# The first image's Gram sums: outer rows turned on TensorE, inner rows in 32-channel blocks on VectorE

## The chip, the cores and the metric

The kernel runs on one core of one Trainium2 chip, in one launch. The metric is the device time of that core in microseconds: the median of the runs shown. One further run was taken with the hardware profiler; every view below is of that one.

## The reference, cut to what matters

Eight images `x[b]` of 256 channels and 96 x 96 pixels, all float32, pass two layers, each added to its input:

- layer 0: group norm; three 1x1 convolutions give q, k, v; a 2-D Fourier transform of each; per head (8 heads of 32 channels) q and k are normalized over all frequencies and give a 32 x 32 attention, whose softmax is taken on the real and on the imaginary part; the result is applied to v, transformed back, its absolute value taken, and a last 1x1 convolution applied;
- layer 1: group norm, then linear attention with softplus features.

The kernel never forms the spectra of q and k. It needs, per image, the 256 x 256 sums over pixels of x times x, and of x times the point-mirrored x (row h, column w against row -h, column -w, modulo 96). From those sums the norms and logits of layer 0 follow. This study is about how those two sums are formed for image 0.

## The kernel before

**Two arenas.** `arena0` and `arena1` (128 partitions, two channel halves of 9232 floats) change roles from image to image: `x_of(b)` holds the image, `y_of(b)` the rotated copy that `rotate` makes.

**Sums.** `products` multiplies a pair of turned rows (pixels on partitions, channels along the free axis): for e = row + mirrored row and o = row - mirrored row it adds e'e into `acc[0]` and o'o into `acc[1]`, four matmuls for each block of pixels. A pair of image rows has 96 pixels to a row, so the pixels must first be brought onto the partitions. Two routes exist.

- `first_sums`, image 0: 24 units of two rows each and a last one of one row. `mirrored(u)` (ScalarE) reverses the mirrored rows, `turn(u)` makes eight TensorE transposes into PSUM and two copies (ScalarE, VectorE) into a *place* in an arena, `pair(u)` makes e (GpSimd) and o (VectorE), and `products` is called twice with 96 of 128 partitions filled. Image rows come in naturally, channels on partitions, with long contiguous rows (`first_loads`). The turned rows stay in their places until `rotate(0)` has used them.
- `pair_sums(b)`, images 1 to 7: `load_grouped(b, v)` fetches eight rows and their mirrors with 32 channels on partitions for each of four row pairs, eight DMAs of 192 KB; `turn_blocks(u)` turns them in 32 x 32 blocks on VectorE, two for each u, and after an odd u writes the turned rows out to DRAM (`xtd`, one DMA of 1536 KB) and asks for the group after next; `pair(u)` makes e and o; three calls of `products` for each u use all 128 partitions. A last u = 12 holds row 48 alone (`xtm`). The turned rows have one buffer, `turned(b)`, so the next even u waits until the write to `xtd` is done. `rotate(b)` fetches the turned rows back.

**Rotation.** `rotate(b)` makes 49 steps of TensorE matmuls with a small matrix `tm` (`load_r`: one DMA of 159 KB from the table `rx` for two units of rows), evicted in turn by ScalarE and VectorE. A step is taken whenever the driver at the end of the kernel says `next(turns)`; eleven are taken while image 0's sums are still running, the others between the links of `attention(0)`.

**Order.** Nothing is scheduled automatically: each engine executes its instructions in the order in which the driver's generators emit them, and all DMAs are issued by SyncE's queue (SP) in that order. For image 0 the driver goes round `first_sums`; from the eleventh round it also calls `next(parts)`, that is `tables()` and in it `load_small()`, which issues 28 small loads (`b12`, `bkq4`, `tcol`, `wkq0`, `b3col`, `wo`), and from the sixteenth it also calls `next(turns)`.

Of the kernel before, what the change touches and what calls it, by code (L numbers as in the profile page):

```python
# [73 lines left out]
def two_layer_kernel(ctx: ExitStack, tc: tile.TileContext, x, w1t, b1, w2t, b2, w3, b3, wot, temp,  # L74
# [252 lines left out]
    def finish(stage):  # L327
        for _ in stage:
            pass
# [3 lines left out]
    def release(key):  # L333
        if next(held.get(key, iter(())), None) is None:
            held.pop(key, None)

    N2 = 2 * C
    places = [(0, 0, 3328), (0, 0, 4864), (0, 1, 4864),
              *((0, k, o) for k, o in ((0, 1280), (0, 2304), (0, 5888), (0, 6912), (1, 5888), (1, 6912))),
              *((1, k, 0) for k in range(KC)), *((0, 1, o) for o in (1280, 2304)), *((1, k, o) for o in (8192, 1024, 7168, 2048, 6144, 3072) for k in range(KC))]  # L340

    def place(u):

# [3 lines left out]
    def first_loads():  # L347

        nc.sync.dma_start(out=t0[:, 0:2 * W], in_=tmat[0, :, W:3 * W])
        x0 = x_of(0)  # L350

        def load(lo, hi):
            nc.sync.dma_start(out=x0[:, :, lo * W:hi * W], in_=x_v[0, :, :, lo * W:hi * W])

        for lo, hi in ((0, 4), (H - 4, H), (4, 8), (H - 8, H - 4), (8, 16), (H - 16, H - 8)):
            load(lo, hi)
        yield
        load(16, 24)
        yield
        for lo in (H - 24, 24, H - 32):  # L360
            load(lo, lo + 8)
        yield
        for t in range(4, NT // 2):
            load(8 * t, 8 * t + 8)
            load(H - 8 * t - 8, H - 8 * t)
        yield

    def first_sums():

        b = 0  # L370
        x0 = x_of(0)
        acc = [acc_tile(f"acc{c}_{b}") for c in range(2)]
        CB = C + 2
        NU = H // 4
        eos, gs = {}, {}

        xr = x0[:, :, 0:HW].rearrange("p k (h w) -> p k h w", w=W)

        def mirrored(u):

            nr = 2 if u < NU else 1
            g = two.tile([P, CH], F32, tag="v16", name=f"g_{b}_{u}")[:, 0:KC * nr * W].rearrange("p (k r w) -> p k r w", k=KC, r=nr)
            h = H - 2 * u
            parts = [(g, xr[:, :, h:h - nr:-1])] if u else [(g[:, :, r:r + 1], xr[:, :, (H - r) % H:(H - r) % H + 1]) for r in range(nr)]
            for to, v in parts:
                nc.scalar.copy(to[:, :, :, 1:W], v[:, :, :, W - 1:0:-1])
                nc.scalar.copy(to[:, :, :, 0:1], v[:, :, :, 0:1])
            return g

        def turn(u):  # L390

            t = place(u)
            nr = 2 if u < NU else 1
            g = gs.pop(u)
            if u < NU:
                gs[u + 1] = mirrored(u + 1)
            for c in range(2):
                pt = ps_tile(f"x_{b}_{u}_{c}")
                for r in range(nr):
                    for k in range(KC):  # L400
                        v = g[:, k, r, :] if c else xr[:, k, 2 * u + r, :]
                        nc.tensor.transpose(pt[0:W, r * C + k * P:r * C + (k + 1) * P], v, ident)
                copy = nc.vector.tensor_copy if c else nc.scalar.copy
                copy(t[:, c * N2:c * N2 + nr * C], pt[0:W, 0:nr * C])

        def pair(u):

            nr = 2 if u < NU else 1
            eo = ring_tile(f"eo_{b}_{u}")[0:W, 0:2 * nr * CB].rearrange("p (q c n) -> p q c n", q=nr, c=2)
            f, g = (place(u)[:, c * N2:c * N2 + nr * C].rearrange("p (r n) -> p r n", r=nr) for c in range(2))  # L410
            e, o = (eo[:, :, c, 1:C + 1] for c in range(2))
            nc.gpsimd.memset(eo[:, :, :, 0:CB:CB - 1], 1.0 if u < NU else R2)
            if u in (0, NU):
                nc.gpsimd.memset(eo[:, 0, :, 0:CB:CB - 1], R2)
                nc.vector.tensor_scalar_mul(o[:, 0], g[:, 0], R2)
                nc.vector.scalar_tensor_tensor(e[:, 0], in0=f[:, 0], scalar=R2, in1=o[:, 0], op0=ALU.mult, op1=ALU.add)  # L416
                nc.vector.scalar_tensor_tensor(o[:, 0], in0=f[:, 0], scalar=R2, in1=o[:, 0], op0=ALU.mult, op1=ALU.subtract)
                e, o, f, g = (v[:, 1:] for v in (e, o, f, g))
            if u < NU:
                nc.gpsimd.tensor_add(e, f, g)  # L420
                nc.vector.tensor_sub(o, f, g)
            eos[u] = eo

        gs[0] = mirrored(0)
        turn(0)
        turn(1)
        pair(0)
        yield
        for u in range(NU + 1):
            if u + 2 <= NU:  # L430
                turn(u + 2)
            if u < NU:
                pair(u + 1)
            eo = eos.pop(u)
            for q in range(2 if u < NU else 1):
                products(acc, eo, q, W, u == 0 and q == 0, u == NU)
            yield
        s0[b] = acc, weights(b)

    def weights(b):  # L440

# [13 lines left out]
    def pair_sums(b):  # L455

        ready = {}

        def prepare(key, step):
            if key in (("turn", 10), ("pair", 10), ("turn", 11), ("turn", 12)):  # L460
                held[key] = step()
            else:
                finish(step())
# [2 lines left out]
            ready[u] = pair(u)  # L466
            yield

        acc = [acc_tile(f"acc{c}_{b}") for c in range(2)]
        CB = C + 2  # L470

        wrap = two.tile([P, 2 * NB8], F32, tag="wrap", name=f"wrap_{b}")
# [48 lines left out]
                (nc.gpsimd if b and u % 2 else nc.vector).tensor_sub(o, ft, gt)  # L521
            return eo, nq, np_

        finish(turn_blocks(0))
        finish(make(0))
        finish(turn_blocks(1))
        if b:
            finish(make(1))
        yield
        for u in range(NG + 1):  # L530
            eo, nq, np_ = ready.pop(u)
            for q in range(nq):
                if q == 0 and u < NG and u + 1 not in ready:
                    prepare(("pair", u + 1), lambda u=u: make(u + 1))
                if q == 1 and u + 2 <= NG:
                    prepare(("turn", u + 2), lambda u=u: turn_blocks(u + 2))
                if (u, q) == (NG - 1, 1):
                    wl = weights(b)
                products(acc, eo, q, np_, u == 0 and q == 0, u == NG)
                yield  # L540
# [188 lines left out]
    def rotate(b):  # L729
# [5 lines left out]
        def load_r(i):  # L735
            tm = tm_tile(f"tm_{b}_{i}")
            o = (TR if i < NP else 1) * (W + 2) + P - W
            v = rx[i][:, 0:o]
            if b == 0 and i < NP:
                v = v.rearrange("(j q) w -> q j w", q=NQ)  # L740
            nc.sync.dma_start(out=tm[:, 0:o], in_=v)
            return tm
# [3 lines left out]
        slots = [area[0:W, k, o + 4 * C * i:o + 4 * C * (i + 1)].rearrange("p (c m) -> p c m", c=2)  # L746
                 for k, o, n in ((0, LO, 3), (1, LO, 3), (0, LO + 12 * C, 1)) for i in range(n)]
        assert LO + 16 * C <= AW and LO + 12 * C <= LO + NS * CH + 2 * CH
        xts, tms = {}, {}
        at_ = [0]  # L750

        def fetch():

            i = at_[0]
            at_[0] += 1
            if i > G * NG // 2:
                return
            h = 2 * i
            if h // TR not in tms:
                tms[h // TR] = load_r(h // TR)  # L760
            if b == 0:
                xts[i] = place(i).rearrange("p (c m) -> p c m", c=2)
                return
            xts[i] = slots[i % len(slots)]
            if h == N:
                nc.sync.dma_start(out=xts[i][:, 0, 0:C], in_=xtm)
            else:
                v, a = divmod(i, G)
                nc.sync.dma_start(out=xts[i], in_=xtd[:, v, 32 * a:32 * a + 32].rearrange("c j (q m) -> (j q) c m", q=NQ))
# [407 lines left out]

    E = mybir.EngineType
    with tc.manual_schedule(engines={E.PE, E.DVE, E.Pool, E.SP, E.Activation}):
        sums, loads, parts = first_sums(), first_loads(), tables()  # L1180
        fetch, turns = rotate(0)
        next(loads)
        next(parts)
        next(loads)
        next(parts)
        next(loads)
        next(parts)
        finish(loads)
        for i, _ in enumerate(sums):
            if i > 9:  # L1190
                next(parts, None)
            if i > 14:
                next(turns)
        finish(mix(0, attention(0), turns))
        for b in range(B):
            sums = pair_sums(b + 1) if b + 1 < B else iter(())
            weave(images(b), sums)
            weave(layer1(b), sums)
            if b + 1 < B:
                fetch, turns = rotate(b + 1)  # L1200
                mixed = mix(b + 1, attention(b + 1), turns)
                output(b, *l1.pop(b), fetch, sums, mixed)
                finish(mixed)
            else:
                output(b, *l1.pop(b))
# [50 lines left out]
```

## Time and profile before

| what | value |
|---|---|
| median of 3 runs | 2520.37 us (2518.79 to 2521.01) |
| profiled execution, device time | 2519.43 us |
| its span, first to last instruction | 2517.7 us |
| TensorE busy | 2489.2 us (99%) |
| VectorE, ScalarE, GpSimd busy | 70%, 46%, 34% |
| granted TensorE clock, mean | 0.993 |
| image 0's sums on TensorE | from 4.81 us (first transpose) to 102.8 us (last product) |

The span is the profiled execution without 1.7 us around it; the profiled time lies 0.9 us below the median. A TensorE that is 99% busy in the page says that it was hardly ever without an instruction, not that it was at its peak. The stage of the change is the first 104 us of 2517.7, so busy shares of the whole page say little of it: it has to be read in the timeline.

### The profile page before, as it was taken

The page shows a single profiled execution, that of the slowest core. Times are in us where ns is not written, and L with a number is a line of the kernel's source. Part 1 is how long each engine was busy: PE and PEld are TensorE (multiplying, and loading weights), DVE is VectorE, ACT ScalarE, POOL GpSimd, SP SyncE. Part 2 cuts the span into 40 slices and gives each one's busy share as a digit, 9 for nine tenths or more (in the row PEclk, how much of TensorE's full clock was granted, in tenths as well). Part 3 has the DMA queues.
Part 4 walks back from the last instruction along what each step waited for, and adds up shares of the span by engine and source line. Part 5 has one row for each costly group of instructions (what it writes and reads, how often), then busy time and mean ns, then how long its engine had stood idle before and what let it go on. Part 6 is the DMA issues. An engine that isn't in the chain of part 4 may idle for free. (4 is left out here: it accounts for less than half of the span.)

```text
span 2517.7 us, 42049 instructions
## 1 busy us (share of the span) xinstructions
PE 2489.2 (99%) x15936; PEld 1758.1 (70%) x15936; DVE 1774.8 (70%) x3448; ACT 1161.3 (46%) x2045; POOL 860.6 (34%) x820
## 2 busy tenths in 40 slices
PE   9999999999999999999999999999999999999998
PEld 8975777667686667856678566785667757677546
DVE  4467776687856877578775787757877578766776
ACT  3344364443545435354453534435354453634553
POOL 4124513245133442234331353413524135142411
PEclk9999999999999999999999999999999999999997
DMA  7134719456192663917549264683637736296004
GB/s 230 35 129 95 183 62 318 154 126 179 64 340 103 158 153 105 335 70 166 135 161 337 42 167 105 216 284 63 163 86 268 232 63 189 60 312 213 1 7 151
DMA packets 264645, 394.07 MB, mean 157 GB/s; under 512 B 37400, under 2 KB 194300, under 8 KB 264444
## 3 DMA queue, kind: packets, MB, share of 16 engines
q1 hardware_dynamic: 264444, 391.38, 52.5%
q8 instruction: 127, 2.08, 0.3%
q14 instruction: 74, 0.61, 0.1%
HBM read 246.99 MB, written 144.32 MB: 155 GB/s over the span
## 5 line engine op out<-in xcount | busy, mean ns | idle before, releaser
L844 PE MATMUL z<-arena,mz 128*128 128x384 f32 (+1 forms) x2304 | 591.9, 488 | 0.0
L894 POOL TENSOR_TENSOR e<-e 128x768 f32<-128x768 f32 x192 | 348.5, 1815 | 552.7 <-ACT e L893 526.4
L852 PE MATMUL po<-e,wo 128*128 128x384 f32 x1536 | 527.5, 487 | 1.7 <-ACT e L895 1.7
L844 PEld LDWEIGHTS z<-arena,mz 128*128 128x128 f32 (+1 forms) x2304 | 310.1, 163 | 234.7 <-issue 50.5
L450 PEld LDWEIGHTS acc<-eo 128*128 128x128 f32 (+1 forms) x2464 | 390.0, 190 | 86.6 <-issue 32.3
L450 PE MATMUL acc<-eo 128*128 128x257 f32 (+3 forms) x2464 | 441.4, 330 | 1.6 <-DVE eo L416 1.6
L852 PEld LDWEIGHTS po<-e,wo 128*128 128x128 f32 x1536 | 290.0, 190 | 204.7 <-ACT e L895 7.2
L889 DVE TENSOR_TENSOR e<-z,xT 128x768 f32<-128x768 f32 x384 | 361.2, 950 | 64.7 <-PE z L844 63.4
L783 PEld LDWEIGHTS y<-tm,arena 96*128 96x128 f32 x3072 | 360.4, 192 | 38.5 <-issue 23.4
L783 PE MATMUL y<-tm,arena 96*128 96x128 f32 x3072 | 379.0, 278 | 0.4 <-DMA arena<-xtd 0.4
L893 ACT ACTIVATE e<-e 128x1536 f32<-128x1536 f32 x192 | 284.5, 1482 | 173.3 <-DVE e L889 171.1
L895 ACT ACTIVATE e<-e 128x768 f32<-128x768 f32 x192 | 162.0, 844 | 381.9 <-POOL e L894 379.9
L854 DVE TENSOR_TENSOR arena<-arena,po 128x384 f32<-128x384 f32 x384 | 209.4, 551 | 180.4 <-PE po L852 180.1
L520 POOL TENSOR_TENSOR eo<-arena 128x768 f32<-128x768 f32 x77 | 157.3, 2042 | 412.6 <-DVE arena L493 312.1
L1149 POOL TENSOR_TENSOR arena<-arena,po 128x384 f32<-128x384 f32 x180 | 178.2, 1009 | 196.2 <-ACT po L1148 166.8
L789 DVE COPY arena<-y 128x384 f32<-128x384 f32 (+1 forms) x192 | 104.7, 545 | 137.4 <-PE y L783 135.9
L789 ACT COPY arena<-y 128x384 f32<-128x384 f32 (+1 forms) x200 | 94.5, 473 | 227.8 <-PE y L783 204.8
L295 DVE BATCH_NORM_STATS2 st<-arena 128x6 f32<-128x384 f32 x384 | 195.2, 548 | 0.6
L1148 ACT COPY po<-o 128x384 f32<-128x384 f32 x180 | 78.0, 482 | 191.0 <-PE o L1140 187.6
L493 DVE STREAM_TRANSPOSE arena<-arena 128x768 f32<-128x768 f32 x168 | 155.2, 956 | 10.2 <-DMA xtd<-arena 8.1
L1009 PE MATMUL xT<-ident,arena 128*128 128x128 f32 x1152 | 144.1, 275 | 1.3 <-ACT xT L1012 1.3
L1009 PEld LDWEIGHTS xT<-ident,arena 128*128 128x128 f32 x1152 | 127.1, 141 | 19.0 <-issue 16.5
(242 smaller groups left out, 2544.7 us busy)
## 6 DMA issues: line engine op xcount, KB each, us to landing
arena<-in_x_dram SPq DMA_DIRECT2D x106, 768.0 KB
out_dram<-arena SPq DMA_DIRECT2D x192, 384.0 KB
xtd<-arena SPq DMA_DIRECT2D x42, 1536.0 KB
arena<-xtd SPq DMA_DIRECT2D x168, 384.0 KB
arena<-in_x_dram SPq DMA_DIRECT2D x329, 192.0 KB
tm<-rx SPq DMA_DIRECT2D x96, 159.0 KB
wl<-in_w1t_dram SPq DMA_DIRECT2D x8, 256.0 KB
wl<-in_w2t_dram SPq DMA_DIRECT2D x8, 256.0 KB
```

The costliest lines, as they stand in the source:

```text
L295: nc.vector.bn_stats(out=st[:, k, c, :], in_=x_of(b)[:, k, c * CH:(c + 1) * CH])
L450: nc.tensor.matmul(acc[c][:, m * (C + 1):m * (C + 1) + C + 1 - m * P], lhsT=eo[0:np_, q, c, 1 + m * P:1 + (m + 1) * P], rhs=eo[0:np_, q, c ...
L783: nc.tensor.matmul(pu[:, o:o + P], lhsT=xt[:, s, k * P:(k + 1) * P], rhs=tm[:, n:n + P], start=True, stop=True)
L789: copy(y[:, :, :, g:g + nr, :], v.rearrange("p k r (f w) -> p k f r w", f=2))
L844: nc.tensor.matmul(out[:, 0:CH].rearrange("p (h q) -> p h q", q=PR), lhsT=columns(mz, k, c, j), rhs=yz[:, k, f, :, o:o + PR], start=(k == ...
L852: nc.tensor.matmul(po[:, 0:CH], lhsT=wo[:, k, m * P:(m + 1) * P], rhs=e[:, k, :], start=(k == 0), stop=(k == KC - 1))
L854: nc.vector.tensor_add(x[:, m, n], x[:, m, n], po[:, 0:CH])
L889: nc.vector.tensor_add(e[:, 2 * c:2 * c + 2, :].rearrange("p t (q h) -> p t q h", h=H), pz[:, 0:CH].rearrange("p (h q) -> p q h", h=H).uns ...
L893: nc.scalar.activation(e, e, AF.Square)
L894: nc.gpsimd.tensor_add(e[:, 0:2, :], e[:, 0:2, :], e[:, 2:4, :])
L1009: nc.tensor.transpose(pt[:, j * C + k * P:j * C + (k + 1) * P], x[:, k, o:o + P], ident)
L1149: nc.gpsimd.tensor_add(x[:, m, r], x[:, m, r], t)
```

## The change

Image 0 now takes both routes. The outer 24 rows and their mirrors go the way of `first_sums` (12 units); the inner rows go the way of `pair_sums(0)`, beginning at u = 6 and adding into the same `acc`. Natural rows of the upper half lie at a shifted address (`LO`), so that the front of the arena is free for the grouped rows. Three places move. In `rotate(0)`, units 12 to 24 are fetched back from `xtd` and `xtm` into five slots. The driver interleaves the first steps of `pair_sums(0)` with the last four rounds of `first_sums`, and small loads and rotation steps with the rest. The diff, with the plain renamings left out:

```diff
@@ places, first_loads
+    V0 = 3
...
-              *((1, k, 0) for k in range(KC)), *((0, 1, o) for o in (1280, 2304)), *((1, k, o) for o in (8192, 1024, 7168, 2048, 6144, 3072) for k in range(KC))]
+              (1, 0, LO), (1, 1, LO), (1, 0, 8192)]
+    NU = V0 * G
...
         def load(lo, hi):
-            nc.sync.dma_start(out=x0[:, :, lo * W:hi * W], in_=x_v[0, :, :, lo * W:hi * W])
+            o = LO if hi <= H // 2 else 0
+            nc.sync.dma_start(out=x0[:, :, o + lo * W:o + hi * W], in_=x_v[0, :, :, lo * W:hi * W])
...
-        load(16, 24)
+        load(16, 2 * NU)
         yield
-        for lo in (H - 24, 24, H - 32):
-            load(lo, lo + 8)
+        load(H - 2 * NU + 1, H - 16)
+        load_grouped(0, V0)
         yield
-        for t in range(4, NT // 2):
-            load(8 * t, 8 * t + 8)
-            load(H - 8 * t - 8, H - 8 * t)
+        load_grouped(0, V0 + 1)
         yield
@@ first_sums
-        acc = [acc_tile(f"acc{c}_{b}") for c in range(2)]
+        acc = s0[b] = [acc_tile(f"acc{c}_{b}") for c in range(2)]
-        NU = H // 4
...
-        for u in range(NU + 1):
-            if u + 2 <= NU:
+        for u in range(NU):
+            if u + 2 < NU:
                 turn(u + 2)
-            if u < NU:
+            if u + 1 < NU:
                 pair(u + 1)
             eo = eos.pop(u)
-            for q in range(2 if u < NU else 1):
-                products(acc, eo, q, W, u == 0 and q == 0, u == NU)
+            for q in range(2):
+                products(acc, eo, q, W, u == 0 and q == 0, False)
             yield
-        s0[b] = acc, weights(b)
@@ pair_sums
+        u0 = 0 if b else 2 * V0
...
-        acc = [acc_tile(f"acc{c}_{b}") for c in range(2)]
+        acc = [acc_tile(f"acc{c}_{b}") for c in range(2)] if b else s0[0]
...
-        finish(turn_blocks(0))
-        finish(make(0))
-        finish(turn_blocks(1))
-        if b:
-            finish(make(1))
+        for step in (turn_blocks(u0), make(u0), turn_blocks(u0 + 1)):
+            finish(step)
+            if b == 0:
+                yield
+        finish(make(u0 + 1))
         yield
-        for u in range(NG + 1):
+        for u in range(u0, NG + 1):
@@ rotate
-            if b == 0 and i < NP:
+            if b == 0 and i < NU // 2:
                 v = v.rearrange("(j q) w -> q j w", q=NQ)
...
+        if b == 0:
+            slots = [area[0:W, k, o:o + 4 * C].rearrange("p (c m) -> p c m", c=2)
+                     for k, o in ((0, LO + 4 * C), (1, LO + 4 * C), (0, LO + 8 * C), (1, LO + 8 * C), (1, LO + 12 * C))]
...
-            if b == 0:
+            if b == 0 and i < NU:
                 xts[i] = place(i).rearrange("p (c m) -> p c m", c=2)
                 return
@@ driver
-        sums, loads, parts = first_sums(), first_loads(), tables()
+        sums, rest, loads, parts = first_sums(), pair_sums(0), first_loads(), tables()
...
         for i, _ in enumerate(sums):
-            if i > 9:
+            if NU - 5 < i < NU:
+                next(rest)
+            if i > 10:
                 next(parts, None)
-            if i > 14:
+        for i, _ in enumerate(rest):
+            next(parts, None)
+            if i > 7:
                 next(turns)
```

More of the change, by code (lines that the diff above doesn't have):

```diff
@@ L337, in two_layer_kernel @@
     N2 = 2 * C
+    V0 = 3
     places = [(0, 0, 3328), (0, 0, 4864), (0, 1, 4864),
               *((0, k, o) for k, o in ((0, 1280), (0, 2304), (0, 5888), (0, 6912), (1, 5888), (1, 6912))),
-              *((1, k, 0) for k in range(KC)), *((0, 1, o) for o in (1280, 2304)), *((1, k, o) for o in (8192, 1024, 7168, 2048, 6144, 3072) for k in range(KC))]
+              (1, 0, LO), (1, 1, LO), (1, 0, 8192)]
+    NU = V0 * G
+    assert len(places) == NU and TO + 2 * NQ * C <= LO and LO + 2 * NU * W <= (H - 2 * NU + 1) * W
     def place(u):
@@ L371, in first_sums @@
         x0 = x_of(0)
-        acc = [acc_tile(f"acc{c}_{b}") for c in range(2)]
+        acc = s0[b] = [acc_tile(f"acc{c}_{b}") for c in range(2)]
         CB = C + 2
-        NU = H // 4
         eos, gs = {}, {}
-        xr = x0[:, :, 0:HW].rearrange("p k (h w) -> p k h w", w=W)
+        xf = x0[:, :, LO:LO + 2 * NU * W].rearrange("p k (h w) -> p k h w", w=W)
+        xg = x0[:, :, 0:HW].rearrange("p k (h w) -> p k h w", w=W)
         def mirrored(u):
-            nr = 2 if u < NU else 1
+            nr = 2
             g = two.tile([P, CH], F32, tag="v16", name=f"g_{b}_{u}")[:, 0:KC * nr * W].rearrange("p (k r w) -> p k r w", k=KC, r=nr)
             h = H - 2 * u
-            parts = [(g, xr[:, :, h:h - nr:-1])] if u else [(g[:, :, r:r + 1], xr[:, :, (H - r) % H:(H - r) % H + 1]) for r in range(nr)]
+            parts = [(g, xg[:, :, h:h - nr:-1])] if u else [(g[:, :, 0:1], xf[:, :, 0:1]), (g[:, :, 1:2], xg[:, :, H - 1:H])]
             for to, v in parts:
@@ L392, in turn @@
             t = place(u)
-            nr = 2 if u < NU else 1
+            nr = 2
             g = gs.pop(u)
-            if u < NU:
+            if u + 1 < NU:
                 gs[u + 1] = mirrored(u + 1)
@@ L400, in turn @@
                     for k in range(KC):
-                        v = g[:, k, r, :] if c else xr[:, k, 2 * u + r, :]
+                        v = g[:, k, r, :] if c else xf[:, k, 2 * u + r, :]
                         nc.tensor.transpose(pt[0:W, r * C + k * P:r * C + (k + 1) * P], v, ident)
@@ L406, in pair @@
         def pair(u):
-            nr = 2 if u < NU else 1
-            eo = ring_tile(f"eo_{b}_{u}")[0:W, 0:2 * nr * CB].rearrange("p (q c n) -> p q c n", q=nr, c=2)
+            nr = 2
+            eo = ring_tile(f"xo_{b}_{u}")[0:W, 0:2 * nr * CB].rearrange("p (q c n) -> p q c n", q=nr, c=2)
             f, g = (place(u)[:, c * N2:c * N2 + nr * C].rearrange("p (r n) -> p r n", r=nr) for c in range(2))
             e, o = (eo[:, :, c, 1:C + 1] for c in range(2))
-            nc.gpsimd.memset(eo[:, :, :, 0:CB:CB - 1], 1.0 if u < NU else R2)
-            if u in (0, NU):
+            nc.gpsimd.memset(eo[:, :, :, 0:CB:CB - 1], 1.0)
+            if u == 0:
                 nc.gpsimd.memset(eo[:, 0, :, 0:CB:CB - 1], R2)
@@ L418, in pair @@
                 e, o, f, g = (v[:, 1:] for v in (e, o, f, g))
-            if u < NU:
-                nc.gpsimd.tensor_add(e, f, g)
-                nc.vector.tensor_sub(o, f, g)
+            nc.gpsimd.tensor_add(e, f, g)
+            nc.vector.tensor_sub(o, f, g)
             eos[u] = eo
@@ L428, in first_sums @@
         yield
-        for u in range(NU + 1):
-            if u + 2 <= NU:
+        for u in range(NU):
+            if u + 2 < NU:
                 turn(u + 2)
-            if u < NU:
+            if u + 1 < NU:
                 pair(u + 1)
             eo = eos.pop(u)
-            for q in range(2 if u < NU else 1):
-                products(acc, eo, q, W, u == 0 and q == 0, u == NU)
+            for q in range(2):
+                products(acc, eo, q, W, u == 0 and q == 0, False)
             yield
-        s0[b] = acc, weights(b)
     def weights(b):
@@ L457, in pair_sums @@
         ready = {}
+        u0 = 0 if b else 2 * V0
         def prepare(key, step):
-            if key in (("turn", 10), ("pair", 10), ("turn", 11), ("turn", 12)):
+            if b and key in (("turn", 10), ("pair", 10), ("turn", 11), ("turn", 12)):
                 held[key] = step()
```

## The prediction

> **What bounds the kernel now.** I read the engine totals, then the stage table for the first 100 us, then TensorE's timeline there, and last SP's timeline and waits.
>
> ```profile
> PE 2489.2 (99%) x15936; PEld 1758.1 (70%) x15936; DVE 1774.8 (70%) x3448; ACT 1161.3 (46%) x2045; POOL 860.6 (34%) x820
> ```
>
> ```profile
> 0.00:10.00 10.00, 5.41 (x28) 4.32 (x28) 4.18 (x33) 5.79 (x18) 4.43 (x63) 1.00 0.81 276
> ...
> 50.00:60.00 10.00, 10.00 (x71) 9.36 (x70) 3.72 (x6) 2.78 (x10) 4.69 (x6) 1.00 0.23 59
> 60.00:70.00 10.00, 10.00 (x73) 9.44 (x71) 4.28 (x8) 3.13 (x9) 3.56 (x5) 1.00 0.12 41
> ```
>
> The stage table (PE, PEld, DVE, ACT, POOL, clock, DMA share, GB/s) shows TensorE full from 20 us on and all else half idle: here TensorE's work is the time. TensorE's timeline gives the price of a unit:
>
> ```profile
> 4.81 1.09 PE L402 MATMUL x<-ident,arena 128*96 128x128 f32 x4 [0.42 <-DMA arena<-in_x_dram]
> ...
> 59.29 0.60 PE L402 MATMUL x<-ident,arena 128*96 128x128 f32 x4
> 59.73 0.60 PE L402 MATMUL x<-ident,g 128*96 128x128 f32 x4
> 60.17 2.79 PE L450 MATMUL acc<-eo 96*128 96x257 f32 x16
> 62.80 1.06 PE L783 MATMUL y<-tm,arena 96*128 96x128 f32 x8
> ```
>
> From start to start, eight transposes take 0.88 us, two calls of `products` 2.63 (1.31 each), a rotation step 0.89. The first rotation step runs at 62.80. Its matrix comes over SP's queue, whose waits tell how that queue moves:
>
> ```profile
> SPq L223 <- DMA tm<-rx: 4.4, 3, 1.9
> ...
> SPq L215 <- DMA arena<-in_x_dram: 3.2, 2, 2.1
> ```
>
> `wo` does not need `tm`, nor `tcol` an image: in the program as built SP's DMAs share eight completion semaphores in turn, so a DMA is issued only once the eighth before it has landed. SP's timeline:
>
> ```profile
> 45.70 3.18 SPq L215 DMA_DIRECT2D tcol<-in_temp_dram  x2
> ...
> 51.13 2.85 SPq L223 DMA_DIRECT2D wo<-in_wot_dram  x8
> 54.02 2.29 SPq L741 DMA_DIRECT2D tm<-rx  x3
> 56.35 2.95 SPq L223 DMA_DIRECT2D wo<-in_wot_dram  x6
> ```
>
> `tm` was issued 8.8 us ahead of need. Of those six `wo` the last, at 59.03, had waited for the first `tm`: 4.9 us from issue to landing.
>
> [...]
>
> **TensorE's work.** Before: 24 units and a last row, 24 x 2.63 + 1.31 = 64.4 us of products and 196 transposes of 0.11, 21.6; together 86.0. After: 12 units, 31.6; six u of three calls and the last one, 19 x 1.31 = 24.9; 96 transposes, 10.6; together 67.1. The 128-row products are priced as the 96-row ones: 24 records at 251.59 us in `pair_sums(1)` take 4.10, three calls of 1.31 and a tail. **Saved: 18.9 us**, all on the path. Two further image loads less, evictions and mirrors less, lie beside TensorE: nothing.
>
> **VectorE and GpSimd.** A u costs VectorE two block transposes of 0.96, one o of 0.96, and every second u two wrap copies of some 0.7: 3.2 us against 3.94 of products. GpSimd's e takes 1.84. Neither bounds while TensorE works. The eight preparatory steps of u = 6, 7 fit in VectorE's 2.2 us gaps of each unit: its last transpose for u = 7 ends at about 46.0 (the copy of unit 11 at 42.86 and two o's come before). In GpSimd e for u = 7 ends at 48, needed at 54.
>
> **Fetching x in blocks.** Of 12 image loads of 768 or 384 KB eight remain; 4.7 MB come in 30 DMAs. At 212 us, sixteen grouped DMAs are issued back to back and then paced by their semaphores, one per 0.93 us, the first landing 2.05 after issue. Two groups by 48 us, behind the `rt` table and the `rx` writes, replace 4.8 MB that had landed by 45: cover is the twelve units, which run to 50.5. Group 3 is put ahead of the `rx` writes on SP; SP waited for the table until 25.65 anyway. GpSimd issues no DMAs; its `b12` memset moves behind e for u = 7, still ahead of the `b12` loads.
>
> **The write to `xtd` and what queues behind it.** This decides. At 260.72 such a write is issued, and the next group's first load is issued at 265.95: 5.2 us to landing. The built program makes odd groups wait for it (a tile of both channel halves is taken as one span of addresses), even ones not.
>
> ```profile
> 260.72 0.38 SPq L498 DMA_DIRECT2D xtd<-arena  x1
> 265.95 0.33 SPq L152 DMA_DIRECT2D arena<-in_x_dram  x1
> ```
>
> In the change, SP's order from 46 us is: write 3, group 5 (eight), `b12` x4, `bkq4` x2, `tcol` x2, `wkq0` x2, `b3col`, `wo` x9, write 4, group 6 (six small), `wo` x8, and only then the first `tm`. Step by step:
> - write 3 issued 46.1, landed 51.6 (the tail of group 4 costs 0.3);
> - group 5 issued from 51.7; its last lands 2.05 + 8 x 0.93 = 9.5 later, 61.2; the second `tcol` uses that semaphore and waits for it;
> - from the second `tcol` to `tm` the trace of before has 54.02 - 48.35 = 5.7 us; 66.9;
> - write 4 and six loads directly behind it: at 318.45 that series took until 323.81, 5.4; 72.3;
> - eight more `wo`, 2.85: `tm` issued at 75.1, landed 4.9 later, at **80.0**.
>
> TensorE ends its twelve units at 11.06 + 9 x 3.51 + 3 x 2.63 = 50.5 (first product at 11.06; the last two units have no transposes) and reaches the first step three u later, 50.5 + 9 x 1.31 = 62.3. It waits 17.7 us; ten calls of `products` and ten steps queue behind. [...] Left to do: step one 0.89, ten calls 13.1, ten steps 8.4 (one is half a step). End 80.0 + 1.5 + 22.4 = 103.9; without a wait it would be 62.3 + 22.4 = 84.7. Before, the same eleven steps and all products end at 103.7 (102.80 plus one step). **Net: +0.2 us**: what is saved goes into one wait.
>
> Write 4 lands at 72.3, so u = 10 is ready at 77, long before its turn. Write 5 follows u = 11 (after VectorE's copy of step two, some 84): landed 91; u = 12 ready by 94, needed at 101.
>
> **Reading back.** Thirteen fetches of 384 KB are added in the attention stage. Five slots let fetch i go when step 2i - 9 is done; it is needed at step 2i, seven us later. Two fetches and a `tm` are 0.95 MB; images 1 to 7 move them at 250 GB/s (stage at 430 us), 3.7 us for four steps of 3.6, with TensorE waiting there 0.4 us in all. I take nothing. The reloads of x for `images(0)`, issued at 148.97 before, no longer wait for places; they were first used at 163, so that is no gain. If the cover fails, each late fetch shows as a wait of L787.
>
> **Sum.** Work -19.0 (103.7 to 84.7), wait +17.7[...]: +0.2 us, on 2519.43 of the profiled execution. The median of the runs stands 0.9 above; the forecast against it is 2520.37 + 0.2, **2520.6 us**. A measurement of this kernel can tell about 0.2%, 5 us, from no change.
>
> **The rivals.**
> 1. *The matrix is in time (faster).* For: its data need nothing of the new work. If `tm` lands by 62.3 the whole 18.9 remain: 2501.5. Between, each microsecond by which it is earlier than 80 is one gained; faster by over 5 us means landing before 75. That needs the small loads to run at their bare issue price, or group 5 to land by 56. Against: the sum from 61.2 to 75.1 is already made of measured pieces without waits. Chance 0.17, typically -9: 2511.
> 2. *The first fetches are late (slower).* Place: DMA between 25 and 47 us. Group 3 must be in by 37, when VectorE turns u = 6, and group 4 must be out of write 3's way. Grouped packets moved 192 KB in 0.93 us, 211 GB/s, natural rows around 28 us 390 and more; if the queue clears only at 53, write 3 lands at 58 and the chain shifts 6 us: 2527. It decides from a landing of `tm` at 85 on. For: semaphores make groups 3 and 4 wait for the table and for `rx`. Chance 0.25, with reading back, if its seven us were missed by 1 us on each of ten fetches, +10, as its far end.
> 3. *It does not do what it says.* If the wait were on blocks rather than on the matrix (VectorE late by a write each time), the first wait would stand at L450 for u = 8 or 10. My times have u = 8 ready at 55.5 against 58.4 and leave that few chances; it gives the same end, since the steps come in order anyway.
>
> **The numbers.** Same 0.58, faster 0.17, slower 0.25. The unknowns: end of VectorE's preparation +-1.5, landings +-1.5, small loads +-2[...]; from these alone +-5. To hold 8 in 10, the range reaches into both rivals: 2511 to 2529.
>
> **What would show it.** Right: in TensorE's timeline one long wait, 12 to 23 us, just before the first L787, released by the DMA `tm<-rx`; L404 96 records instead of 196; SP issuing `tm` near 75; write 3 near 46 and group 5's first load 5 us after it; L450 ending near 103. Wrong: no wait there, or a wait at L450 for `eo` released by VectorE or GpSimd (then preparation, not SP, bounds); waits at L787 after 110 us (then reading back); TensorE's first long wait before 50 us (then the first fetches).

## The result and the profile after

The changed kernel takes **2526.32 us** (median of ten runs, 2523.62 to 2528.44); the kernel before, in ten runs beside it, 2520.18 (2518.79 to 2521.20). The ratio is 1.0025, with a 95% interval of 1.0016 to 1.0033: slower by a quarter of a per cent. The profiled execution of after took 2523.62 us, the fastest of its ten, with a span of 2521.8 against 2517.7: 4.1 us longer.

First the engine totals of the page (busy time, share, instructions), beside which 2489.2 us and 15936 stood for PE before:

```profile
PE 2468.3 (98%) x15788; PEld 1735.1 (69%) x15788; DVE 1778.7 (71%) x3450; ACT 1148.4 (46%) x2007; POOL 856.8 (34%) x806
```

TensorE is busy 20.9 us less, and the span is 4.1 us longer. Only 16.7 of the 20.9 belong to the change: by the stage table TensorE is busy for 98.35 us of the first 104 before, and for 81.63 us of the first 108 after. The other 4.2 lie behind 160 and 164 us, where both kernels do the same and take the same 2358 us. One group of instructions (over the whole span) and TensorE's waits in the first 200 us say in one line each where the time went (the group's last columns are the idle time just before its instructions, and what ended it):

```profile
L787 PE MATMUL y<-tm,arena 96*128 96x128 f32 x3072 | 379.9, 278 | 20.7 <-DMA tm<-rx 20.7
```

```profile
PE y L787 <- DMA tm<-rx: 20.7, 1, 20.7
```

One wait of 20.7 us, for the matrix of the first rotation step. TensorE's timeline puts it in its place (start, length, line, operation, count, and in brackets the idle time before):

```profile
50.79 11.99 PE L450 MATMUL acc<-eo 128*128 128x257 f32 x72
83.47 2.05 PE L787 MATMUL y<-tm,arena 96*128 96x128 f32 x8 [20.70 <-DMA tm<-rx]
85.31 2.35 PE L450 MATMUL acc<-eo 128*128 128x257 f32 x8
87.50 0.61 PE L787 MATMUL y<-tm,arena 96*128 96x128 f32 x4
87.94 1.48 PE L450 MATMUL acc<-eo 128*128 128x257 f32 x8
...
106.91 6.42 PE L787 MATMUL y<-tm,arena 96*128 96x128 f32 x56
```

Nine calls of `products` for u = 6, 7, 8 run without a gap and end at 62.77. The last line begins with the eleventh step, so products and eleven steps end at 106.91 + 0.89 = 107.8, where before had 103.7: 4.1 later, which is the whole difference of the spans. Reading back cost nothing: TensorE waits for no fetch up to the first matmul of `images(0)`, and this starts again 4.1 us later. Here are the eleventh step and that matmul in TensorE's timeline of before, then the matmul in that of after:

```profile
102.80 6.42 PE L783 MATMUL y<-tm,arena 96*128 96x128 f32 x56
...
152.10 10.72 PE L844 MATMUL z<-arena,mz 128*32 128x384 f32 x56
```

```profile
156.21 10.72 PE L848 MATMUL z<-arena,mz 128*32 128x384 f32 x56
```

SP's timeline shows the chain to `tm`:

```profile
47.70 0.39 SPq L499 DMA_DIRECT2D xtd<-arena  x1
52.93 0.31 SPq L152 DMA_DIRECT2D arena<-in_x_dram  x1
...
63.04 1.10 SPq L215 DMA_DIRECT2D tcol<-in_temp_dram  x2
...
69.34 0.39 SPq L499 DMA_DIRECT2D xtd<-arena  x1
...
74.72 3.47 SPq L223 DMA_DIRECT2D wo<-in_wot_dram  x8
78.23 1.53 SPq L742 DMA_DIRECT2D tm<-rx  x2
```

Write 3, group 5, the small loads, write 4 with group 6, more small loads, and at 78.23 the first `tm`. In this trace each of SP's 1133 DMAs carries the completion semaphore of the eighth before it, and the wait for that one can be read off: the third and fourth `b12` were issued at 58.12 and 59.09, and the loads of group 5 eight places ahead of them had landed at 58.10 and 59.07. The step that needs this `tm` starts 5.2 us after its issue; it was wanted at 62.77. That step and the products behind it are slow as well, and the stage table (PE, PEld, DVE, ACT, POOL, clock, DMA share, GB/s) tells why:

```profile
60.00:63.00 3.00, 2.77 (x18) 2.36 (x16) 0.00 (x0) 0.00 (x0) 0.37 (x2) 1.00 0.71 114
66.00:70.00 4.00, 0.00 (x0) 0.00 (x0) 0.00 (x0) 0.00 (x0) 0.00 (x0) 0.58 0.27 58
...
80.00:83.40 3.40, 0.00 (x0) 0.00 (x0) 0.00 (x0) 0.00 (x0) 0.00 (x0) 0.50 0.19 62
83.40:85.40 2.00, 1.93 (x9) 1.96 (x10) 0.00 (x0) 0.00 (x0) 0.00 (x0) 0.50 0.14 53
85.40:87.50 2.10, 2.10 (x10) 1.79 (x9) 0.00 (x0) 0.54 (x2) 0.00 (x0) 0.60 0.01 4
87.50:90.00 2.50, 2.50 (x21) 2.39 (x20) 1.86 (x4) 0.00 (x0) 0.00 (x0) 1.00 0.00 0
```

In this run the granted clock falls to half 3.8 us after the last matmul (0.58 over four us: 0.6 us of them full) and is still at half when `tm` comes. An array at half clock is called cold here. Step one takes 1.84 us from start to start instead of 0.89, the products behind it 2.19 instead of 1.31, together 1.8 us.

### The profile page after: what moved, and what is told of

Its sections match the earlier page's. It is cut to its first block, busy times and chain, and to the rows that moved or that the text cites. A ratio compares the mean times of both kernels' runs of the same rounds, so it can differ in the third digit from the quotient of the medians.

```text
span 2521.8 us, 41724 instructions
## 1 busy us (share of the span) xinstructions
PE 2468.3 (98%) x15788; PEld 1735.1 (69%) x15788; DVE 1778.7 (71%) x3450; ACT 1148.4 (46%) x2007; POOL 856.8 (34%) x806
## 5 line engine op out<-in xcount | busy, mean ns | idle before, releaser
L450 PEld LDWEIGHTS acc<-eo 128*128 128x128 f32 (+1 forms) x2224 | 353.6, 190 | 81.6 <-issue 32.3
L787 PEld LDWEIGHTS y<-tm,arena 96*128 96x128 f32 x3072 | 361.2, 192 | 58.8 <-issue 45.4
L450 PE MATMUL acc<-eo 128*128 128x257 f32 (+3 forms) x2224 | 400.6, 331 | 0.0
L787 PE MATMUL y<-tm,arena 96*128 96x128 f32 x3072 | 379.9, 278 | 20.7 <-DMA tm<-rx 20.7
L521 POOL TENSOR_TENSOR eo<-arena 128x768 f32<-128x768 f32 x83 | 172.3, 2076 | 447.4 <-DVE arena L494 346.9
L494 DVE STREAM_TRANSPOSE arena<-arena 128x768 f32<-128x768 f32 x180 | 166.2, 955 | 20.8 <-DMA xtd<-arena 18.5
```

Source lines behind the costliest of these rows:

```text
L450: nc.tensor.matmul(acc[c][:, m * (C + 1):m * (C + 1) + C + 1 - m * P], lhsT=eo[0:np_, q, c, 1 + m * P:1 + (m + 1) * P], rhs=eo[0:np_, q, c ...
L787: nc.tensor.matmul(pu[:, o:o + P], lhsT=xt[:, s, k * P:(k + 1) * P], rhs=tm[:, n:n + P], start=True, stop=True)
```

## The experiments

Two theories stood against each other. **Order:** SP's order makes `tm` late; with `tm` earlier in it, the wait goes. **Blocks:** the inner rows are late by themselves, and a wait for them would take the place of the wait for `tm`. Times are medians, with before at 2519.2 to 2520.1 on the same chip, unless a run is said to be a single one.

**e1: the first two `tm` ahead of write 3.**

```diff
@@ driver, rounds of first_sums
+            if i == NU - 4:
+                for _ in range(4):
+                    fetch()
```

> The changed kernel with one edit: the first two rotation matrices (tm) are asked for before write 3 to xtd, so they stand ahead of group 5 and of all small loads in SP's queue. Nothing else moves. Theory (SP's order makes the wait): no wait at L787 any more. But write 4 still stands behind the small loads, at some 70 us, so u = 10 is ready only near 79 and TensorE waits some 9 us at L450 instead, from 70; [...] the sums and eleven steps end near 96 instead of 107.8: span 2509.6, 12 less than the changed kernel, some 10 less than before. Rival (the grouped loads and block turning are what is late, tm only the first to show it): the wait moves whole to L450, 18 us or more, span 2519 to 2522.

Measured: 2518.37 us, ratio to before 0.9993 (0.9985 to 1.0001), span 2516.9. The wait at L787 is gone, and two at L450 stand in its place, in TensorE's timeline:

```profile
64.20 6.29 PE L450 MATMUL acc<-eo 128*128 128x257 f32 x24 [5.40 <-POOL eo L509]
...
85.67 2.94 PE L450 MATMUL acc<-eo 128*128 128x257 f32 x8 [8.11 <-POOL eo L509]
```

Order holds for `tm`; Blocks holds for what comes next, and the time is nearer to what Blocks expected. The releaser POOL is only the last of a row (GpSimd makes e when VectorE has turned the blocks); SP's timeline has the cause:

```profile
48.46 0.40 SPq L499 DMA_DIRECT2D xtd<-arena  x1
59.52 0.33 SPq L152 DMA_DIRECT2D arena<-in_x_dram  x1
```

Behind the two `tm`, write 3 took 11.1 us to land, and 11.1 again in e3; with `tm` elsewhere in the order it took 5.2 to 7.1 (5.2 in after, up to 6.8 when after was profiled again), and u = 8 needs its buffer. Some of the delay is not due to `tm`: group 4 was asked for 3 us later than in after (41.55 against 38.50) and was still coming in when the write was issued. The expected wait at u = 10 came; the one at u = 8 had not been foreseen.

**e2: all small loads but `b12` behind the last write.** In the rounds of `pair_sums(0)`:

```diff
-            next(parts, None)
+            if i > 11:
+                next(parts, None)
...
+        finish(parts)
```

> The changed kernel with the other edit alone: tm stays where it is, but of the small loads only those of b12 are left between group 5 and write 4; the others (bkq4, tcol, wkq0, b3col, wo) come after the last write. Theory: write 4 leaves when group 5 has landed, near 63 instead of 69, tm is issued near 69 and lands near 74: a wait of 11 us at L787, end near 98.5, span 2512.5. Rival (small loads cost nothing, the big transfers ahead of tm do): tm lands no earlier than 80, wait 18 us or more, span above 2518.

Measured: 2528.41 us, ratio 1.0032 (1.0019 to 1.0045), span 2526.6.

```profile
76.06 2.05 PE L787 MATMUL y<-tm,arena 96*128 96x128 f32 x8 [12.86 <-DMA tm<-rx]
...
111.43 2.05 PE L787 MATMUL y<-tm,arena 96*128 96x128 f32 x8 [4.81 <-DMA tm<-rx]
```

The first wait fell from 20.7 to 12.9, so about eight of its microseconds were the small loads in front. But moved back, they stand in front of later `tm`, and a second wait arises, behind which the steps are slow again: four take 6.63 us from 116.12 on, where four just ahead of the wait took 3.81. The first part of the expectation held, the time did not.

**e3: both edits together.**

> Both edits: tm ahead of write 3, small loads after the last write. Theory: TensorE waits only for u = 10, whose turning waits for write 4 (issued near 63.5, landed near 68.7): 2 to 3 us at L450, then nothing; end of sums and eleven steps near 87.5, so that 16 of the 19 us of saved work are kept: span 2501.5, about 0.65% faster than the kernel before. Rival (something else of the new route, such as GpSimd's or VectorE's share or reading back in the attention stage, bounds next): end later than 95 or new waits at L787 after 110 us; span 2508 or more.

Measured: 2523.15 us, ratio 1.0011 (1.0005 to 1.0018), span 2521.3. 20 us were expected of it and did not come: waits of 4.7 and 3.1 us for u = 8 and 10, and again one for a later `tm`, after which the array stays slow, in TensorE's timeline and then in the stage table:

```profile
106.71 2.05 PE L787 MATMUL y<-tm,arena 96*128 96x128 f32 x8 [5.18 <-DMA tm<-rx]
...
111.40 6.61 PE L787 MATMUL y<-tm,arena 96*128 96x128 f32 x32
```

```profile
111.00:114.00 3.00, 3.00 (x16) 3.00 (x16) 0.93 (x5) 0.77 (x3) 0.00 (x0) 0.50 0.24 81
114.00:118.00 4.00, 4.00 (x24) 3.88 (x25) 0.63 (x2) 0.58 (x3) 0.00 (x0) 0.59 0.49 136
```

Four steps take 6.61 us, in after 3.82. TensorE is without a gap from 106.71 on and yet at half clock until about 117.3 (0.59 over four us: 0.7 us of it full), so a wait of 5.2 us cost some 5 more (an estimate: half of the 10.6 us from 106.71 to 117.3).

**e4: write 3 in two DMAs, one for each channel half,** so that group 5 need not wait for the whole.

```diff
-                nc.sync.dma_start(out=xtd[:, v].rearrange("c p m -> p c m"), in_=x_of(b)[:, :, TO:TO + 2 * NQ * C])
+                for c in range(2):
+                    nc.sync.dma_start(out=xtd[c, v], in_=x_of(b)[:, c, TO:TO + 2 * NQ * C])
```

> The changed kernel with the write to xtd cut in two DMAs, one for each channel half, for all images; then group 5 need not wait for write 3. Theory: group 5 is issued right behind write 3 [...], its last load lands near 61 instead of 63 to 63.5, and tm comes 2 to 3 us earlier: wait 18 instead of 20.7 us, span near 2519.3 (the other images unchanged). If waiting for write 3 were the main cost, the wait would shrink by its whole 5.2 us, to 15.5; if the wait were of no account, it stays at 20 to 21.

Measured: one run, 2524.38 us, span 2522.6, a wait of 19.7 us at the first step, and `tm` issued at 78.67 (after: 78.23). Group 5 was asked for from 47.93 on instead of 52.93, and yet `tm` came no sooner. That does not show that the wait for write 3 costs nothing, because this run was late before the edit has an effect: group 4 was asked for at 41.51, in the three profiled runs of after at 38.50 to 40.32. From there until group 5 was in it took 22.5 us, against 24.7 to 25.2 in those three: 2.3 to 2.8 us less, about what was expected. One run can't settle it.

**e5 and e8: a warm array,** one that is still at full clock. After, with 82 and then 96 matmuls of the identity, whose result is not used, ahead of the first step (`range(96)` in e8).

```diff
+            if i == 8:
+                pw_ = ps_tile("warm_fill")
+                for _ in range(82):
+                    nc.tensor.matmul(pw_[:, 0:P], lhsT=ident, rhs=ident, start=True, stop=True)
```

> After, with 82 extra matmuls (the 128x128 identity by itself, result unused) put on TensorE just before the first rotation step, so that the array works through most of the 20.7 us wait instead of standing idle. Theory (the first step and the products behind it take 1.8 us more because the array is cold after the wait): the first L787 takes 0.89 instead of 1.84 and the next products 1.31 instead of 2.19; end of image 0's sums 1.8 us earlier, span 2521.8 - 1.8 = 2520.0. Rival (the longer first step is the price of a semaphore wait, not of idleness): step and products as in after, span 2521.8.

> As e5 (82 extra matmuls, which ended 4.5 us before tm landed, and the first step still took 1.84 us) with 96 of them, so that they end at about 84.4, when tm lands at 83.5 to 85.7. Theory (idleness makes the array cold): the first L787 takes 0.89 to 1.1 instead of 1.84 from start to start and the products behind it 1.31 instead of 2.19, with a wait under 2 us left. Rival (the step after any wait for a DMA is slow): 1.84 again. The time itself follows the landing of tm and tells nothing here.

Measured: e5 2526.90 us (ratio 1.0028, 1.0018 to 1.0038), span 2525.3; e8, one run, 2523.05, span 2521.3. In e5 the extra matmuls ended 4.5 us before `tm` came, since SP's chain was later in this run (`tm` issued at 80.32), and the step took 1.84 us again: the run decided nothing on the cold array. In e8 they ended 0.3 us before:

```profile
84.88 1.13 PE L787 MATMUL y<-tm,arena 96*128 96x128 f32 x8 [0.34 <-DMA tm<-rx]
85.84 1.48 PE L450 MATMUL acc<-eo 128*128 128x257 f32 x8
87.16 0.61 PE L787 MATMUL y<-tm,arena 96*128 96x128 f32 x4
```

The step took 0.96 us, the products 1.32, and the clock in the stage table was 1.00 throughout. So it is idleness that makes the step slow, and in after it is worth about 1.8 us: e8 got its `tm` 1.4 us later than after and ends 0.5 sooner.

**e6: the two `tm` directly behind write 3, ahead of group 5.**

```diff
@@ turn_blocks, behind the write to xtd
+                if b == 0 and v == V0:
+                    for _ in range(4):
+                        fetch()
```

> After, with the first two tm asked for directly behind write 3 to xtd and ahead of group 5 (after: behind group 5, the small loads, write 4 and group 6). Theory (SP's order makes the wait; e1 put tm ahead of write 3, which slowed the write): write 3 lands at 52.9 as in after, tm at 54.5 and 56.5, no wait at L787; group 5's last landing moves from about 63.6 to 64 to 66, write 4 from 69.3 to 70 to 71, u = 10 is ready at 79 instead of being needed at 70.3: one wait of 8 to 9 us at L450, and 1.8 us of cold array. End of the sums 84.7 + 8.7 + 1.8 = 95.2 against 107.8, span about 2509.5. Rival (tm slows whatever follows it as it slowed write 3 in e1, by 5.9 us): group 5 lands at 69, write 4 leaves at 75, the wait at L450 is 13, span about 2514.

Measured: 2519.22 us, ratio 0.9996 (0.9988 to 1.0004), span 2517.6. No wait at L787; one for u = 10:

```profile
84.10 2.94 PE L450 MATMUL acc<-eo 128*128 128x257 f32 x8 [14.48 <-POOL eo L512]
```

The rival was nearer (13 us expected, 14.5 came). VectorE could use group 5 at 68.32, 14.6 us after its first load was asked for; in after it had taken 10.6 (52.93 to 63.49). Group 5 took 14.0 to 15.0 in e6, e7 and e9, where the two `tm` stand just ahead of it, and 10.2 to 10.6 in after, e1 and e3, where no `tm` stands next to it. So what stands behind the two `tm` is late: by some 4 us for group 5, and for write 3 in e1 by 4 to 6, a part of which is group 4's. The span was above what either theory had given (2509.5 and 2514).

**e7: as e6, with `wkq0`, `b3col` and `wo` behind write 4 but ahead of write 5.**

```diff
-            next(parts, None)
+            if i == 0 or i > 4:
+                next(parts, None)
```

> As e6, and of the small loads only b12, bkq4 and tcol stay ahead of write 4; wkq0, b3col and wo follow write 4 and group 6, all of them still ahead of write 5 (in e2 they stood behind it and in the way of later tm). Theory: the second tcol is issued at 64 to 66 as in e6 and write 4 directly behind it, 5 us earlier than in e6; u = 10 is ready at 73 to 75, needed at 70.3: a wait of 3 to 5 us and up to 2 us of cold array; write 5 leaves in time. End of the sums about 90.5, span 2504 to 2506. Rival (the moved loads make a later wait again, as in e2 and e3): L787 or L450 waits after 85 us for tm or for u = 12, span 2508 to 2511.

Measured: **2515.28 us**, ratio 0.9981 (0.9973 to 0.9989), span 2514.6: the first version faster than before. The later waits that the rival feared did not come, but the one for u = 10 stayed at 10.2 us instead of 3 to 5:

```profile
80.57 2.94 PE L450 MATMUL acc<-eo 128*128 128x257 f32 x8 [10.21 <-POOL eo L512]
```

Group 5 was in at 68.41, write 4 could leave at 69.16, as late as in after (69.34), though only eight small loads stood between instead of twenty. The `tm` ahead of group 5 took back what the small loads gave.

**e9: as e7, with eight of the eleven steps taken before u = 10 and three behind u = 11;** steps 2 to 7 are evicted by ScalarE alone.

```diff
-            if i > 7:
+            for _ in range({8: 1, 9: 1, 10: 2, 11: 4, 17: 3}.get(i, 0)):
                 next(turns)
...
-            copy = (nc.scalar.copy, nc.vector.tensor_copy)[i % 2]
+            copy = (nc.scalar.copy, nc.vector.tensor_copy)[i % 2 if b or not 2 <= i < 8 else 0]
```

> As e7, with rotation steps moved in time, not in number: eight of the eleven are taken before u = 10 (e7: four), the other three between u = 11 and u = 12; of the first eight, steps 2 to 7 are evicted by ScalarE alone, since VectorE's queue stands at u = 10. Theory (e7 stands 10.2 us at u = 10 with work to do that needs nothing of it): the wait falls by four steps of 0.9, to 6.6 us; u = 10 begins at 80.6 as before; tm for step 8 lands at 90 and u = 12 is ready at 92.6, so the sums end at 94 instead of 98.1. Span 2514.6 - 4 = 2510.5. Rival (the third tm or u = 12 is late): a wait before step 8 or u = 12 takes back what is won, span 2513 to 2515.

Measured: **2512.41 us**, ratio 0.9974 (0.9965 to 0.9983), span 2510.0, as expected (2510.5); of the rival's late `tm` 1.7 us came. No work is taken away; it is put where TensorE stood idle:

```profile
70.14 3.74 PE L790 MATMUL y<-tm,arena 96*128 96x128 f32 x32
81.01 9.85 PE L450 MATMUL acc<-eo 128*128 128x257 f32 x48 [7.13 <-POOL eo L512]
92.53 2.92 PE L790 MATMUL y<-tm,arena 96*128 96x128 f32 x24 [1.67 <-DMA tm<-rx]
```

**e10: as e9, with the two `tm` behind group 5 instead of ahead of it,** and all eight early steps behind u = 9 (`{11: 8, 17: 3}`).

> As e9, with the first two tm directly behind group 5 instead of ahead of it, and all eight early steps after u = 9. Theory (in e6 and e7 the two tm ahead of group 5 made its landing 5 us later): group 5 lands at 63 to 64 as in after, write 4 leaves at 65 and lands at 71, u = 10 is ready at 75; tm lands at 66 to 68, just when u = 9 ends (66.7); eight steps fill 67 to 75; write 5 leaves at 80, tm for step 8 lands at 86, u = 12 ready at 89, sums end at 91. Span about 2507.5. Rival (the two tm cost the queue the same wherever they stand): write 4 leaves at 69 as in e7, u = 10 begins at 80, span 2510 to 2511.

Measured: 2512.32 us, ratio 0.9973 (0.9962 to 0.9985), span 2511.4: the same time as e9. Group 5 was in at 65.12, four us sooner than in e9, and the first step found its `tm` at 66.31 without a wait. But write 4 left at 68.53, 1.4 us sooner than in e9, not five: the eighth DMA before the second `tcol` is now the second `tm`, and the two `tcol` took 2.71 us to issue, in after 1.10. Most of what was won at u = 10 (it begins at 79.30) is lost at step 8, where `tm` is late by 2.4 us and the steps behind it are slow again (three take 4.24 us, in e9 2.92):

```profile
91.48 4.24 PE L790 MATMUL y<-tm,arena 96*128 96x128 f32 x24 [2.44 <-DMA tm<-rx]
```

So it is the rival that came (2510 to 2511 expected, 2511.4 measured). The two `tm` cost the queue nearly the same on either side of group 5.

**e11 and e12: after, unchanged, profiled again.** The ten runs of after spread over 4.8 us, those of before over 2.4.

> After unchanged, profiled once more: its ten runs spread over 4.8 us (2523.6 to 2528.4), those of before over 2.4, and the profiled one was the fastest. Theory (the landing of the first tm at the end of SP's chain differs from run to run, as in e5, where the same order of DMAs had tm issued 2.1 us later, and TensorE's end follows it): first L787 between 83.5 and 87, and the time is 2523.6 + (its start - 83.47), within 0.7 us. Rival (the spread arises elsewhere): L787 at 83.5 again with a time of 2526 to 2528, or a later L787 with no later end.

> As e11, a second time: again the time should be 2523.6 + (start of the first L787 - 83.47), within 0.7 us.

Measured: 2525.68 and 2525.72 us, one run each; the first step starts at 84.63 and 84.97, which by the rule gives 2524.8 and 2525.1. So 1.2 and 1.5 us of the 2.1 by which they are above the profiled run are the later landing. `images(0)` starts at 158.07 and 158.03, 1.9 later than in that run, so nearly the rest lies in the same stage, in a longer time at half clock (5.1 and 4.3 us of work, in after 3.6; in e11 the first products take 2.57 us from start to start instead of 2.19, then a half step 0.76 instead of 0.44). The rule was right in direction and 0.6 to 0.9 us short, where 0.7 had been allowed. Only 0.2 to 0.3 us of the difference lie behind `images(0)`.

SP's timelines show where the lateness begins (start of each, and the start of the first step on TensorE):

| | after | e11 | e12 |
|---|---|---|---|
| table read back from `rt` | 12.28 | 12.79 | 13.00 |
| first write to `rx` | 28.99 | 29.88 | 30.46 |
| group 4 asked for | 38.50 | 39.80 | 40.32 |
| group 5 asked for (write 3 landed) | 52.93 | 53.91 | 54.42 |
| `tm` issued | 78.23 | 79.58 | 79.74 |
| first step | 83.47 | 84.63 | 84.97 |

The delay is there before any turned row is written out: it is the first fetches, behind the table and the `rx` writes, that are later.

## Why the prediction was right, and where it was off

**The mechanism was right.** One long wait stands just before the first L787, released by `tm`; L402's 196 transposes became 96; TensorE came to the first step at 62.77 (predicted 62.3); neither the attention stage nor the first fetches made a wait of TensorE's. The 18.9 us of TensorE's work are really saved: after without its wait and its cold clock would end at 107.8 - 20.7 - 1.8 = 85.3 instead of 103.7, 18.4 us; and the 16.7 us by which TensorE was busy for less are 18.5 when the 1.8 of the cold clock are added. e9 says so from the other side: its profiled run took 2511.83 us, with waits of 7.1 and 1.7 and some 1.8 for its cold array (an estimate: half of its 3.5 us of work at half clock), which leaves 2501.2. The prediction put the case without a wait at 2501.5; from e9's own before, 2519.24, its 18.9 us would lead to 2500.3. That the wait came out about as long as the saved work is a coincidence of this order: nothing ties the two together.

**The sizes were off, all in one direction,** and so the forecast of no change (2520.6) was 5.7 us short: the result lies in its range of 2511 to 2529, but 6.1 us above before, and by the prediction's own line of 5 us that is "slower" (chance 0.25) and not the favoured "same" (0.58). Step by step, in the profiled run:

| step | predicted | measured | late by |
|---|---|---|---|
| write 3 issued | 46.1 | 47.70 | 1.6 |
| write 3 landed | 51.6 | 52.93 | 1.3 |
| second `tcol` | 61.2 | 63.6 | 2.4 |
| write 4 issued | 66.9 | 69.34 | 2.4 |
| last eight `wo` begin | 72.3 | 74.72 | 2.4 |
| `tm` issued | 75.1 | 78.23 | 3.1 |
| `tm` landed (first step) | 80.0 | 83.47 | 3.5 |

Three terms carry it. First, VectorE's preparation: one of the o that I had priced at 0.96 us took 2.56 while GpSimd's e of the same block was running, and so the last transpose ended at 47.7 and not at 46.0. These are GpSimd's e and VectorE's o for u = 6, then o and e for u = 8, from the two timelines:

```profile
40.73 2.69 POOL L521 TENSOR_TENSOR eo<-arena 128x768 f32<-128x768 f32 x1 [2.23 <-DVE arena L494]
41.68 2.56 DVE L522 TENSOR_TENSOR eo<-arena 128x768 f32<-128x768 f32 x1
...
54.88 0.96 DVE L522 TENSOR_TENSOR eo<-arena 128x768 f32<-128x768 f32 x1
54.92 2.60 POOL L521 TENSOR_TENSOR eo<-arena 128x768 f32<-128x768 f32 x1 [3.72 <-DVE arena L494]
```

Where e was well under way, o was long; where they began together, o took its 0.96 and e 2.6 instead of 1.84. What decides which of the two is held up was not tried, and the order alone doesn't tell: at 48.17 an o begun 0.35 us after its e took 0.94, and the e 2.97. Second, group 5 with its small loads took 1.1 us more than sixteen grouped loads back to back had suggested. Third, the last `wo` took 3.5 instead of 2.85. The parts without a wait in between (second `tcol` to write 4, write 4 to `wo`: 5.7 and 5.4) came out to a tenth. The cold array cost 1.8; the 1.5 in the prediction's 80.0 + 1.5 + 22.4 was my estimate for slow work behind the wait, and the profile of before had not shown its size. Nor is the time at half clock the same from run to run: 3.6 us of work in after (83.47 to about 87.1), 6.0 in e7 and 10.6 in e3.

**The step from the profile to the median was wrong.** I carried over the 0.9 us by which before's profiled run lies below its median. After's lies 2.7 below, because a chain of DMAs is now on the path, and its landing differs from run to run: 83.47, 84.63, 84.97, and 85.76 in e5, which has the same order. Before had no wait for that chain, and its spread showed nothing of it. So of the 5.7 us by which the forecast was short, 3.9 are the sizes above (the end of the sums at 107.8 instead of 103.9), and the other 1.8 are the difference of these two steps from profile to median.

**Rivals.** The first (the matrix in time) is what e1, e6 and e7 made true, and they showed what the prediction didn't: with `tm` in time the next wait stands at L450 for u = 8 or 10, and by the medians 14.6 to 18.5 of the 18.9 us are given back. The prediction's "u = 10 is ready at 77, long before its turn" was true only because TensorE was itself late; without the wait its turn comes at about 70 (69.6 in e6, 70.4 in e7). The second (late first fetches) happened in small: in e11 and e12 they put `tm` 1.2 and 1.5 us later, to the edge of the 85 at which that rival was to begin. The third (blocks first) did not happen in after and is the bound of e9 and e10.

What stays open: why two `tm` of together 0.3 MB hold back a transfer behind them by some 4 us or more, and why the return to full clock takes 3.5 us of work in one place (e9) and 10.6 in another (e3). For the first the stage table has a hint: alone on the queue, from 80 to 83.4 in after, the `tm` move 62 GB/s at a DMA share of 0.19, and the landing of write 3 behind them in e3 ends in 4 us (54 to 58) at 55 to 96 GB/s and shares of one to two tenths, after three us at 391 to 425. So `tm` is slow without filling the engines; whether it keeps to a few of them, the views do not show. No run takes the first wait away and leaves everything else in place.

## What to carry to other kernels

Work saved on the busiest engine is worth only as much as the next thing it waits for lets through: read when the engine will reach each later consumer without the saved time, and compare that with the landing of every input, not the first alone. A load that was issued with 9 us in hand was late by 21 once two large writes, two groups of loads and eight more small loads stood ahead of it on the same queue. Moving that load forward alone brought the kernel back to the time of before and no further (e1, e6), and moving all small loads to the end lost (e2). What helped was both, with the small loads behind the write that frees a buffer but still ahead of the next consumer's load (e7), and then filling the wait that remained with work that needs none of it (e9: 6.8 us better than before, some 13 better than after).

## What the runs showed of the hardware that I had not expected

- The granted clock shows a cold array. It fell to half 2.6 us (e7) to 3.8 us (after, e9) after the last matmul. The waits of 0.3 us (e8) and 1.7 us (e9) left it at 1.00; after those of 5.2 us (e3), 7.1 (e9), 10.2 (e7) and 20.7 (after) work began at 0.50. Behind the 2.4 us in e10 three steps took 4.24 us, in e9 2.92. The clock then stayed at half for 3.5 us (e9), 3.6 (after) to 6.0 us (e7) of work, and for 10.6 in e3, where nearly all of the work behind the wait was rotation steps. Half of that time is what such a wait cost on top of itself: an estimate of 1.8 to 3 us, and 5.3 in e3.
- Two small transfers (0.33 MB together) in front of a write of 1.5 MB went with 11.1 us to its landing instead of 5.2 to 7.1; in front of group 5 they made that 14.0 to 15.0 instead of 10.2 to 10.6.
- The same program's DMA chain landed at times up to 1.5 us apart in three profiled runs (83.47, 84.63, 84.97). Off the path before's spread showed nothing of it; on the path it is most of the 2.1 us between these runs.
